# Layer 0's parameters turned by 18 transfers; layer 1's norm and statistics moved to ACT and PE, one more third of delta·x to DVE; setup transfers issued from two queues

## The chip, the cores and the metric

The kernel runs on one core of one Trainium2 chip. A core has TensorE (PE), VectorE (DVE), ScalarE (ACT), GpSimd (POOL) and SyncE (SP); SP issues nearly all transfers here. The metric is the device time in microseconds (us). The kernel before takes 19113.97 us, the median of three runs from 19105.77 to 19115.89. A smaller time is better.

## What is computed

Two blocks follow each other on 32 images of 96 channels and 56 x 56 pixels, all in float32.

- Layer 0 is an inverted bottleneck: a 1x1 convolution to 576 channels, a 3x3 depthwise convolution, squeeze-and-excite, a 1x1 convolution back to 96 channels, and the input added. Its weights are rounded to 8 bits first ("fake quant"), and its three batch norms are folded to a scale and a shift per channel.
- Layer 1 reads each image as a sequence of 3136 positions and passes it through two Mamba layers. A final 1x1 convolution is normalised over all images and positions, and layer 0's output is added again.

```python
h = (seq - mu) * rsqrt(var + EPS) * ln_g + ln_b      # per position, over 96 channels
xs, z = split(h @ in_w)                              # 192 channels each
xc = silu(causal conv of 4 taps of xs)
dt, Bm, Cm = split(xc @ xproj_w)                     # 6, 16, 16
delta = softplus(dt @ dt_w + dt_b)                   # 192 channels
hstates = scan: h = exp(delta*A) * h + delta*Bm*xc   # 192 x 16 states
y = (sum over states of hstates*Cm + Dp*xc) * silu(z)
seq = seq + y @ out_w
```

## The kernel before

The program has two phases and a short ending.

**Layer 0** takes up the first 3460 us. Weights and parameters come into SBUF, are quantised (`fake_quant`) and folded (`bn_fold`). The depthwise convolution on PE leaves the four 32-channel groups of a tile rotated by r groups, so whatever is multiplied with its result has to be rotated too: `turned` copies the scale `inv2`, the shift `sh2`, the bias `SEB2`, the weights `w3` and `sew1` with one transfer for every 32-row block. `folded` does the like for the last, half-filled tile. SP issues all of them, and behind them the first images (`load_x`). Then a loop over the images runs in an order written out by hand.

**Layer 1** is cut into units: 784 positions (`LC`) of one of 128 pieces, in one of the 2 Mamba layers, 256 units in all. A unit has 24 steps (`NT`), one for each group of 32 channels and 4 states: 192 x 16 / 128. In the order written out by hand (`manual_schedule`), each step `at` issues, engine by engine:

- `inject` (POOL): bx = u x B, for two steps at once, four steps ahead of its use.
- `decay` (ACT): da = exp(delta x A) for the next step, into one of two PSUM buffers.
- `scan` (DVE): the recurrence, for one step; `product` (DVE) multiplies 512 of the 784 columns with C for two steps at once, and `rest` (POOL) the other 272. `bring` (ACT) brings C into PSUM for `product`.
- `save` (ACT): the last state, one column for each step, if the image goes on.
- `reduce` (PE): sums the states, five steps later; `gated` (DVE) multiplies with silu(z).

Between these stand the steps of other units: `prepare(n)` has the norm, projections, convolution, delta and u of a unit, spread over the steps from -4 to 36 counted from 48 steps ahead of its own scans, so that its step 36 is issued beside step 12 of the unit ahead of it. `finish(n)` projects a finished unit and stores it. A number with a fraction in the list, such as 34.5, puts the step ahead of the scan of the next whole step. Work that waits for something holds up what is behind it on its engine.

The parts that the change touches are these. `center` subtracts the mean (PE). `square` copies the centred sequence to `xm` and squares it (ACT). `variance`, `root` and `newton` make the reciprocal root `rs`, with positions on partitions. `spread_root` lays it along the columns by a multiplication with the identity (PE), and `normalise` multiplies `xm` with it (DVE, two instructions). `conv` (PE) reads the result `xn`. `softplus` makes delta and writes it to HBM; `input_u` (POOL) multiplies two of three parts of delta and x, and `bring_x` (ACT) and `input_u0` (DVE) the first one. `spread` writes u to HBM, and `fetch` reads delta, u, B and C back, spread over the partitions as the scan wants them. `store` and `count` write a unit of the second Mamba layer to HBM, with `bn_stats` (DVE) for the last norm.

Between the two phases stands layer 1's setup, where `pieces` yields the blocks of weights that are loaded one by one from SP. All memory of layer 1's work tiles is taken up from what the setup leaves.

Of the kernel before, what the change touches and what calls it, by code (L numbers as in the profile page):

```python
# [11 lines left out]
F32 = mybir.dt.float32  # L12
AF = mybir.ActivationFunctionType
# [40 lines left out]
def conv_mamba_kernel(ctx, tc, a, out):  # L54
# [24 lines left out]
    stats = const.tile([C, B * NQ * 2, 6], F32, name="stats", tag="stats")  # L79
# [16 lines left out]
    with ExitStack() as ph:  # L96
# [19 lines left out]

        hp = loadw("hp", [128, NCT, NHP])
        w1 = loadw("w1", [C, HID])
        w3 = loadw("w3", [128, NCT, C])
        sew1 = loadw("sew1", [128, NCT, RED])  # L120
# [19 lines left out]

        fake_quant(w1, C, [HID], "w1")
# [6 lines left out]


        def turned(name, t, shape):  # L150
            to = wtile(name, [128, NSEE, *shape])
            for e, (ct, r) in enumerate(SEEN):
                if ct == FOLD:
                    parts = [(slice(h * 64, h * 64 + 64), slice(0, 64)) for h in range(2)]
                elif r == 0:
                    parts = [(slice(0, 128), slice(0, 128))]
                else:
                    parts = [
                        (slice(q * 32, q * 32 + 32), slice((q - r) % 4 * 32, (q - r) % 4 * 32 + 32)) for q in range(4)
                    ]  # L160
                for rows, src in parts:
                    sp.dma_start(to[rows, e], t[src, ct])
            return to
# [11 lines left out]

        tinv = turned("tinv", inv2.unsqueeze(2), [1])
        tsh = turned("tsh", sh2.unsqueeze(2), [1])
        tseb = turned("tseb", hp[:, :, SEB2 : SEB2 + 1], [1])
        tw3 = turned("tw3", w3, [C])
        tsew1 = turned("tsew1", sew1, [RED])  # L180
# [24 lines left out]

        xs, maps, h2s, pools, se = {}, {}, {}, {}, {}

        def load_x(b):
            if b < B:
                xs[b] = xin.tile([C, L], F32, name=f"x{b}", tag="x")  # L210
                sp.dma_start(xs[b], a["x"][b])
# [193 lines left out]
        load_x(0)  # L405
        load_x(1)
# [42 lines left out]
    with ExitStack() as ph:  # L449
# [9 lines left out]
        def loadw(name, shape, pool=wts):  # L459
            t = pool.tile(list(shape), F32, name=name, tag=name)  # L460
            sp.dma_start(t, a[name])
            return t
# [17 lines left out]
        def pieces():  # L480

            for m in range(DIN // DB):
                hc, c0 = divmod(m * DB, C)
                for h in range(2):
                    r0 = h * 64 + m % 2 * DB
                    yield slice(r0, r0 + DB), m // 2, h, slice(c0, c0 + DB), hc
# [3 lines left out]
        for to, k, h, src, hc in pieces():  # L490
            sp.dma_start(outw[to, :, k, :], a["outw"][src, :, hc, :])
            sp.dma_start(dp[to, :, k, :], a["dp"][src, :, hc, KC + 1 : KC + 3])

        araw = loadw("acol", [128, NL, NT], once)
# [48 lines left out]
        for to, k, h, src, hc in pieces():  # L543
            sp.dma_start(wbc[to, :, k, : 2 * NS], a["xpw"][src, :, hc, RANK:])
            sp.dma_start(wbc[to, :, k, 2 * NS : 2 * NS + RANK], a["xpw"][src, :, hc, :RANK])
        for h in range(2):
            for i in range(NL):
                to = wd[h * 64 + 2 * NS : h * 64 + 2 * NS + RANK, i, :, :]
                sp.dma_start(to, a["dtw"][:, i, :].rearrange("r (k m) -> r k m", k=NB))
# [27 lines left out]
        nch = B * NQ  # L577

# [17 lines left out]
        def prepare(n):  # L596
# [18 lines left out]
            def square(h):  # L615
                if h == 0:
                    d["xm"] = wt([C, LC], "xm", 1, n)
                    d["sq"] = wt([C, LC], "sq", 1, n)
                s.copy(d["xm"][:, cols(h)], d["cen", h][:C, :HB])
# [32 lines left out]
            def spread_root(h):  # L652
                ps = d["rstd", h] = bank(f"rstd_{n}_{h}")
                for k in range(NK):
                    lo, hi = max(k * TK, h * HB), min((k + 1) * TK, h * HB + HB)
                    if lo < hi:
                        pe.matmul(
                            ps[:C, lo - h * HB : hi - h * HB], d["rs"][:, k : k + 1].to_broadcast([TK, C]),
# [3 lines left out]
            def normalise(h):  # L662
                to = xn[:C, KC - 1 + h * HB : KC - 1 + h * HB + HB]
                v.tensor_mul(to, d["xm"][:, cols(h)], d["rstd", h][:C, :HB])  # L664
# [50 lines left out]
            def spread(tag, t):  # L715
# [310 lines left out]
```

## Time and profile before

| | |
|---|---|
| median of the runs | 19113.97 us |
| the profiled execution's own time | 19128.83 us |
| its span, first to last instruction | 19127.1 us |
| busy over the span | DVE 94%, POOL 81%, PE 76%, ACT 74% |
| first matmul | 112.40 us |
| scans of layer 1 | from 3563.98 us to 18828 us |
| mean granted TensorE clock | 0.816 |

Busy shares over the whole span mix stages with different limits. In the stretch from 6,000 to 12,000 us, which is layer 1 alone, DVE is busy for 5927.62 us, POOL for 5993.50, ACT for 4963.45 and PE for 4461.17. A row of groups tells an operation by its line, engine and tiles (out<-in), how many there were, the busy time, the mean length in ns, the idle time of the engine just before them and what ended that idle time. A row of a timeline has the start and the length in us, and in brackets the idle time before it. Instructions on one engine overlap a little at their ends, so the distance from start to start is what counts in a sum.

### The profile page before, as it was taken

Reading aid. Unit: us, or ns where it says so; the run is one execution under the profiler, and the core shown is the slowest. Engines: PE = TensorE matmul, PEld = TensorE weight load, DVE = VectorE, ACT = ScalarE, POOL = GpSimd, SP = SyncE. Lnnn points to the kernel's source line nnn. Section 1 sums busy time; section 2 is a strip of 40 time slices with the busy share of each in tenths; the row PEclk is TensorE's granted clock in tenths of the full one; section 3 lists DMA queues with packets and bytes.
Section 4 is the critical chain, followed back from the end, with each engine's and each line's share of the span. In section 5 each row is a group of like instructions: output and inputs, shape, how many; then the busy total and the mean of one; then the engine's idle time right before and its main releaser. Section 6 shows DMA issues by size and latency. Waiting matters only on the chain.

```text
span 19127.1 us, 282833 instructions
## 1 busy us (share of the span) xinstructions
PE 14494.5 (76%) x105692; PEld 5826.8 (30%) x105692; DVE 17929.2 (94%) x13652; ACT 14174.0 (74%) x23979; POOL 15533.5 (81%) x6638
## 2 busy tenths in 40 slices
PE   7999999777777777777777777777777777777772
PEld 3544444322222222222222222222222222222220
DVE  7888888699999999999999999999999999999993
ACT  3444444588888888888888888888888888888884
POOL 0000000599999999999999999999999999999994
PEclk9999999778777777877777787778878787777775
DMA  1000000355555555555555555555555555555557
GB/s 27 22 27 23 26 27 20 105 162 162 162 162 162 164 163 162 162 162 162 162 162 163 162 163 163 163 163 162 164 162 162 163 163 163 162 163 163 163 162 207
DMA packets 1048524, 2641.35 MB, mean 138 GB/s; under 512 B 129080, under 2 KB 342416, under 8 KB 1041000
## 3 DMA queue, kind: packets, MB, share of 16 engines
q1 hardware_dynamic: 1040488, 2584.73, 42.4%
q0 software_dynamic: 6656, 38.54, 1.0%
q8 instruction: 828, 13.57, 0.3%
q14 instruction: 552, 4.52, 0.1%
HBM read 2172.52 MB, written 449.58 MB: 137 GB/s over the span
## 4 chain that ended last, share of the span: by engine, by line
DVE 37%; issue 33%; ACT 21%; PE 5%; POOL 3%; SPq 1%; DMA 1%; POOLq 0%; DVEq 0%; ACTq 0%
DVE hh L864 20%; DVE hc L872 12%; ACT da L832 5%; ACT L588 4%; ACT L589 3%; DVE h L303 2%; ACT cp L840 2%; PE bc L701 2%; POOL bx L852 1%; ACT z L588 1%; ACT dl L588 1%; ACT xc L588 1%; PE var L625 1%; DVE z L915 1%; POOL x L378 1%
## 5 line engine op out<-in xcount | busy, mean ns | idle before, releaser
L852 POOL TENSOR_TENSOR bx<-ub,B 128x1568 f32<-128x1568 f32 x3072 | 10983.4, 3575 | 26.0 <-DMA ub<-ud 15.5
L864 DVE TENSOR_TENSOR_SCAN hh<-da,state,bx 128x784 f32<-128x784 f32 x4608 | 8315.7, 1839 | 47.5 <-ACT da L832 41.6
L832 ACT ACTIVATE da<-deltab,acol 128x784 f32<-128x784 f32 x6144 | 5631.1, 917 | 2159.5 <-DVE hh L864 2125.6
L879 POOL TENSOR_TENSOR hc<-hh,C 128x544 f32<-128x544 f32 x3072 | 4217.7, 1373 | 31.4 <-DVE hh L864 23.5
L676 PE MATMUL xs<-xn,wx 97*64 97x392 f32 x12288 | 2892.5, 607 | 1362.9 <-DVE xn L664 1362.3
L872 DVE TENSOR_TENSOR hc<-hh,cp 128x1024 f32<-128x1024 f32 x3072 | 3679.7, 1198 | 0.1
L904 PE MATMUL y<-hc,rel 128*32 128x392 f32 x24576 | 3008.2, 577 | 366.8 <-DVE hc L872 348.2
L378 POOL TENSOR_TENSOR x<-x,x 96x784 f32<-96x784 f32 x128 | 268.4, 2097 | 3180.1 <-ACT x L377 3142.2
L864 DVE TENSOR_TENSOR_SCAN hh<-da,bx 128x784 f32<-128x784 f32 x1536 | 2682.5, 1778 | 53.3 <-ACT da L832 34.2
L676 PEld LDWEIGHTS xs<-xn,wx 97*64 97x64 f32 x12288 | 1303.2, 164 | 2972.9 <-DVE xn L664 1672.6
L840 ACT COPY cp<-C 128x512 f32<-128x512 f32 x3072 | 1793.7, 584 | 372.9 <-DVE hc L872 371.1
L303 DVE SCALAR_TENSOR_TENSOR h<-hpad,hp,h 128x1568 f32<-128x1568 f32 x1024 | 2035.0, 1987 | 34.3
L701 PE MATMUL bc<-xc,wbc 64*64 64x392 f32 x3072 | 980.8, 802 | 646.7 <-ACT xc L588 646.7
L904 PEld LDWEIGHTS y<-hc,rel 128*32 128x32 f32 x24576 | 579.7, 115 | 2090.6 <-issue 1139.4
L277 PE MATMUL dw<-hpad,diag 32*32 32x392 f32 x36864 | 1113.0, 522 | 47.4 <-issue 47.1
L692 PE MATMUL z<-xn,wz 97*64 97x392 f32 x3072 | 741.2, 563 | 487.7 <-ACT xc L687 472.7
L375 PE MATMUL c<-h,w3s 128*96 128x392 f32 (+1 forms) x2560 | 968.0, 523 | 48.8 <-DVE w3s L360 48.8
L588 ACT ACT_TABLE_LOAD x768 | 985.3, 1283 | 13.5
L589 ACT ACT_TABLE_LOAD x768 | 985.3, 1283 | 11.2
L224 PE MATMUL c<-x,w 96*128 96x392 f32 x2048 | 801.9, 548 | 198.8 <-DMA x<-in_x_dram 112.4
L284 ACT ACTIVATE h<-dw,tsh,tinv 128x392 f32<-128x392 f32 x512 | 340.0, 673 | 755.8 <-PE dw L277 755.8
L774 PE MATMUL o<-z,outw 64*96 64x392 f32 x3072 | 802.9, 656 | 101.2 <-DVE z L915 100.5
(156 smaller groups left out, 15566.8 us busy)
## 6 DMA issues: line engine op xcount, KB each, us to landing
deltab<-deltad SPq DMA_DIRECT2D x1536, 392.0 KB, 5.4
ub<-ud SPq DMA_DIRECT2D x1536, 392.0 KB, 5.8
B<-bcd SPq DMA_DIRECT2D x1024, 392.0 KB, 4.2
C<-bcd SPq DMA_DIRECT2D x1024, 392.0 KB, 4.2
deltad<-dl SPq DMA_DIRECT2D x512, 294.0 KB, 3.6
ud<-us SPq DMA_DIRECT2D x512, 294.0 KB, 3.7
x<-in_x_dram SPq DMA_DIRECT2D x32, 1176.0 KB, 7.5
out_dram<-x SPq DMA_DIRECT2D x128, 294.0 KB, 2.6
```

The source lines that it names most:

```text
L303: v.scalar_tensor_tensor(acc, src, tap, acc, ALU.mult, ALU.add)
L588: s.activation(t, t, func)
L589: s.preload_act_table_set(MAIN)
L676: pe.matmul(d["xs", k][h * 64 : h * 64 + 64, :HB], wx[:, i, o, k * 64 : k * 64 + 64], xn[:, o + h * HB : o + h * HB + HB], start=o == 0, s ...
L701: pe.matmul(ps[r, :HB], wbc[r, i, k], d["xc"][r, k, :], start=k == 0, stop=k == NB - 1)
L832: s.activation(das[at][:, :LC], d["delta", k][:, p, :], AF.Exp, scale=acol[:, j, i, 2 * k + p : 2 * k + p + 1])
L840: s.copy(cps[at], data[n]["C", j][:, :LP])
L852: g.tensor_mul(bx, data[n]["u", k], beside(data[n]["B", j]))
L864: v.tensor_tensor_scan(hhs[at - p][:, p, :], das.pop(at)[:, :LC], bxs.pop(at), state[i][:, t : t + 1] if c % NQ else 0.0, ALU.mult, ALU.add,)
L872: v.tensor_mul(hcs[at - 1][:, :, :LP], hhs[at - 1][:, :, :LP], beside(cps.pop(at)))
L879: g.tensor_mul(hcs[at - 1][:, :, LP:], hhs[at - 1][:, :, LP:], beside(data[n]["C", j][:, LP:]))
L904: pe.matmul(yps[k][r0 : r0 + DB, :HB], rel, hc[:, p, h * HB : h * HB + HB], start=False, stop=j == SG - 1, skip_group_check=True,)
```

## The change

- Layer 0: the three folded vectors and the two weights stand side by side in one tile `per` (123 columns), and one loop of 18 transfers turns all of them, at most two blocks a rotation. The first two images are loaded ahead of the quantisation.
- Layer 1's setup: `pieces` yields 8 blocks, not 12, and part of the loads is issued by ACT (`s.dma_start`).
- Layer 1's norm: `turn` multiplies the sequence with the centring matrix so that positions come out on partitions (PE, 7 matmuls); there `rs` is a scale per partition, which `normalise` applies (ACT, 7 instructions); `turn_back` turns it again (PE, in `spread_root`'s place), and `normal` copies it to `xn` (ACT, two). `xm` and its two copies are gone.
- delta x: POOL keeps one third; DVE gets the second as well, by `bring_x(1)` and `input_u(1)`, at steps 38 and 39; `bring_x(0)` moves from step 36 to 34. u is written to HBM in two parts.
- Statistics: ACT takes sums and sums of squares about a pivot with accumulators (`store`); `bn_stats` is gone, and `count` moves from step 19 to 8.
- `save` copies two columns at every second step.

```diff
+        NPER = 3 + C + RED
+        per = wtile("per", [128, NCT, NPER])
+        w3, sew1 = per[:, :, 3 : 3 + C], per[:, :, 3 + C :]
...
+        load_x(0)
+        load_x(1)
+
         fake_quant(w1, C, [HID], "w1")
...
-        def turned(name, t, shape):
-            to = wtile(name, [128, NSEE, *shape])
...
-                    parts = [
-                        (slice(q * 32, q * 32 + 32), slice((q - r) % 4 * 32, (q - r) % 4 * 32 + 32)) for q in range(4)
-                    ]
-                for rows, src in parts:
-                    sp.dma_start(to[rows, e], t[src, ct])
-            return to
+        for o, t in enumerate((inv2, sh2, hp[:, :, SEB2])):
+            v.tensor_copy(per[:, :, o], t)
+
+        turn = wtile("turn", [128, NSEE, NPER])
...
+                parts = [(slice(r * 32, 128), slice(0, 128 - r * 32)), (slice(0, r * 32), slice(128 - r * 32, 128))]
+            for rows, src in parts:
+                sp.dma_start(turn[rows, e], per[src, ct])
...
-            for m in range(DIN // DB):
-                hc, c0 = divmod(m * DB, C)
+            for k, c, o, hc, c0 in ((0, 64, 0, 0, 0), (1, DB, 0, 0, 64), (1, DB, DB, 1, 0), (2, 64, 0, 1, DB)):
...
             sp.dma_start(outw[to, :, k, :], a["outw"][src, :, hc, :])
-            sp.dma_start(dp[to, :, k, :], a["dp"][src, :, hc, KC + 1 : KC + 3])
-
-        araw = loadw("acol", [128, NL, NT], once)
+            s.dma_start(dp[to, :, k, :], a["dp"][src, :, hc, KC + 1 : KC + 3])
+
+        araw = loadw("acol", [128, NL, NT], once, s)
...
-            sp.dma_start(wbc[to, :, k, 2 * NS : 2 * NS + RANK], a["xpw"][src, :, hc, :RANK])
+            s.dma_start(wbc[to, :, k, 2 * NS : 2 * NS + RANK], a["xpw"][src, :, hc, :RANK])
...
-                sp.dma_start(to, a["dtw"][:, i, :].rearrange("r (k m) -> r k m", k=NB))
+                s.dma_start(to, a["dtw"][:, i, :].rearrange("r (k m) -> r k m", k=NB))
...
-                s.copy(d["xm"][:, cols(h)], d["cen", h][:C, :HB])
                 s.activation(d["sq"][:, cols(h)], d["cen", h][:C, :HB], AF.Square)
...
+            def turn(m):
+                ps = d["ct", m] = bank(f"ct_{n}_{m}")
+                for k in TURNS[m]:
+                    o = (k - TURNS[m][0]) * C
+                    pe.matmul(ps[:TK, o : o + C], seqs[c, i][:, k * TK : (k + 1) * TK], cen, start=True, stop=True)
+
+            def normalise(m):
...
+                    s.activation(d["xt"][:, k, :], d["ct", m][:TK, o : o + C], AF.Copy, scale=d["rs"][:, k : k + 1])
+
+            def turn_back(h):
...
-                            ps[:C, lo - h * HB : hi - h * HB], d["rs"][:, k : k + 1].to_broadcast([TK, C]),
+                            ps[:C, lo - h * HB : hi - h * HB], d["xt"][:, k, :],
...
-            def normalise(h):
+            def normal(h):
                 to = xn[:C, KC - 1 + h * HB : KC - 1 + h * HB + HB]
-                v.tensor_mul(to, d["xm"][:, cols(h)], d["rstd", h][:C, :HB])
+                s.copy(to, d["xn", h][:C, :HB])
...
+            def input_u(k):
+
+                if k == NB - 1:
+                    d["us"] = wt([128, NB, HB], "us", 1, n)
+                    g.tensor_mul(d["us"][:, k], d["dl"][:, k], d["xc"][:, k])
+                    return
+                v.tensor_mul(d["us"][:, k], d["dl"][:, k], d["up", k][:, :HB])
+                spread("u", d["us"], slice(0, 1) if k == 0 else slice(1, NB))
...
-                steps += [(8 + h + then, lambda h=h: spread_root(h)), (11 + then, lambda h=h: normalise(h))]
+                steps += [(7 + h + then, lambda h=h: turn(h)), (8 + h + then, lambda h=h: normalise(h))]
+                steps += [(9 + h + then, lambda h=h: turn_back(h)), (10 + h + then, lambda h=h: normal(h))]
...
-            steps += [(26.5 + then, lambda: through(d["z"], AF.Silu)), (34.5 + then, softplus), (35 + then, input_u)]
-            steps += [(36 + then, bring_x), (36 + then, input_u0)]
+            steps += [(26.5 + then, lambda: through(d["z"], AF.Silu)), (34.5 + then, softplus), (35 + then, lambda: input_u(NB - 1))]
+            steps += [(34 + then, lambda: bring_x(0)), (36 + then, lambda: input_u(0))]
+            steps += [(38 + then, lambda: bring_x(1)), (39 + then, lambda: input_u(1))]
...
+                s.activation(
+                    d["pre"][:, cols(h)], d["o", h][:C, :HB], AF.Identity, bias=g2[:, b : b + 1],
+                    accum_out=stats[:, 0, at : at + 1],
+                )
...
+                s.activation(squares, d["pre"][:, cols(h)], AF.Square, bias=pivot, accum_out=stats[:, 1, at : at + 1])
...
-                    for h in range(2):
-                        v.bn_stats(stats[:, 2 * c + h, :], d["pre"][:, cols(h)])
...
-                (6, lambda: store(0)), (7, lambda: store(1)), (19, count),
+                (6, lambda: store(0)), (7, lambda: store(1)), (8, count),
...
-            if c % NQ + 1 < NQ:
-                s.copy(state[i][:, t : t + 1], hh[:, p, LC - 1 :])
+            if place(t)[2] == 1:
+                hh = hhs.pop(at - 1)
+                if c % NQ + 1 < NQ:
+                    s.copy(state[i][:, t - 1 : t + 1], hh[:, :, LC - 1])
...
-        v.bn_aggr(mv, stats.rearrange("p n k -> p (n k)"))
+        off = one.tile([C, 1], F32, name="off", tag="off")
+        v.tensor_reduce(mv, stats, AX.X, ALU.add)
```

## The prediction

> **What bounds the kernel now.** I read the page's groups first, then the waits of layer 1, then the timelines of single engines. Most of the span is layer 1. From 4,000 to 18,500 us the groups count 4,404 + 1,440 scans of DVE, so a unit of 24 scans takes 14,500 / 5,844 x 24 = 59.55 us, and 256 units 15,245 us.
>
> ```profile
> L852 POOL TENSOR_TENSOR bx<-ub,B 128x1568 f32<-128x1568 f32 x243 | 860.0, 3539 | 0.0
> L879 POOL TENSOR_TENSOR hc<-hh,C 128x544 f32<-128x544 f32 x243 | 322.6, 1328 | 0.0
> L726 POOL TENSOR_TENSOR us<-dl,xc 128x784 f32<-128x784 f32 x20 | 36.8, 1839 | 0.0
> ```
>
> These are POOL's groups from 3,800 to 5,000 us, early in layer 1, with no idle time at all. Each instruction begins 0.032 us before its forerunner ends, so a unit costs POOL 12 x (3.539 + 1.328) + 1.839 - 25 x 0.032 = 59.44 us. Later POOL has built up a lead: its bx ends some 4 us ahead of the scan that reads it (it was 1.7 us in the first 16 units), and its hc starts as little as 0.14 us after its scan. So it waits a little for DVE, inside its recorded spans.
>
> ```profile
> DVE us L734 <- ACT up L731: 98.5, 244, 0.5
> DVE hh L864 <- ACT da L832: 63.4, 191, 0.6
> ```
>
> DVE's own waits, 4,000 to 18,500 us: never for POOL, twice per unit for ACT. With two short ones DVE's idle time is 0.72 us a unit, leaving 59.55 - 0.72 = 58.83 us of work. DVE with its waits for ACT sets the pace; POOL's 59.44 is only 0.11 behind. Relieving one alone would win almost nothing.
>
> ```profile
> 10036.45 1.85 DVE L864 TENSOR_TENSOR_SCAN hh<-da,state,bx 128x784 f32<-128x784 f32 x1
> 10038.21 1.01 DVE L664 TENSOR_TENSOR xn<-xm,rstd 96x392 f32<-96x392 f32 x2
> 10039.14 1.84 DVE L864 TENSOR_TENSOR_SCAN hh<-da,state,bx 128x784 f32<-128x784 f32 x1
> 10040.90 1.19 DVE L872 TENSOR_TENSOR hc<-hh,cp 128x1024 f32<-128x1024 f32 x1
> 10042.33 0.56 DVE L734 TENSOR_TENSOR us<-dl,up 128x392 f32<-128x392 f32 x1 [0.24 <-ACT up L731]
> 10042.81 0.56 DVE L915 TENSOR_TENSOR z<-z,y 128x392 f32<-128x392 f32 x1
> ...
> 10058.88 1.01 DVE L789 BATCH_NORM_STATS2 stats<-sq 96x6 f32<-96x392 f32 x2
> 10059.81 1.83 DVE L864 TENSOR_TENSOR_SCAN hh<-da,state,bx 128x784 f32<-128x784 f32 x1
> ```
>
> DVE's timeline: prices from start to start. The xn pair costs 0.93 us (10,039.14 - 10,038.21), us 0.48, a pair of statistics 0.93. A scan costs 1.75 and a product 1.11.
>
> ```profile
> 66.45 18.94 SPq L162 DMA_DIRECT2D tw<-w  x30
> 85.44 19.01 SPq L162 DMA_DIRECT2D tsew<-sew  x30
> 104.49 1.52 SPq L211 DMA_DIRECT2D x<-in_x_dram  x3
> ```
>
> SP's start: 0.63 us for each transfer, the images last; they land at 112.40, where PE's first matmul begins.
>
> **Start: -90 us.** 150 turning transfers become 18, and x is issued behind nine loads, at about 5 us. Landed 7.9 us later (112.40 - 104.49) it is hidden: the first matmul next waits for w1, whose quantisation ends on DVE at 21.48, and three added copies of 128x5 cost 0.15 each. So 112.4 becomes 22.0. What is late next? The turned tile: quantised w3 ends near 24.4, then 18 x 0.63 = 11.3, and 3.7 for a landing (u's stores), in all 39.5. Its first reader, layer 0's first activation of a PE tile, came 20.2 us after the first matmul (132.64 - 112.40), so at 42.2, and needs only 7 of the 18. Were all 3 us later than that, it would cost just the excess.
>
> **Setup of layer 1: -14 us.** SP issued 53 blocks of weights every 0.64 us, acol 25th, at 3476.89; PE's chain from acol (3478.98) to its last setup matmul took 13.4, while the sequence's load went out at 3495.25. Now SP keeps 16 and ACT has 21: acol is ninth on ACT's queue, at about 3463.5 and landed by 3465.5, so PE is done near 3479. The sequence's load waits for this, as it is placed in the setup's memory; 3479 + 3.3 = 3482 in place of 3498.6, less 2 for the longer first norm chain. ACT had 18 us of idle time here, and nothing but acol's exponential queues behind its issues. [...] With transfers as the limit the gain would be 0; but DMA engines are 24% busy from 3,420 to 3,600 us and issues stand 0.64 apart, so issue time is what is short. I take 14, range 0 to 19.
>
> **Loop, DVE.** Out: xn 0.93, statistics 0.93 / 2 = 0.47 (only the second layer has them). In: the second third of u, 0.48. 58.83 - 0.93 - 0.47 + 0.48 = 57.91 us, plus waits for ACT.
>
> **Loop, POOL.** u falls from 784 to 392 columns. 544 columns take 1.328 and 1568 take 3.539, that is 2.16 ns each and 0.15 fixed (784: 1.85, seen 1.84), so 1.00 us; 59.44 - 0.84 = 58.60 us. POOL becomes the longer one.
>
> **Loop, ACT.** It is busy 82% of the loop, some 49 us a unit. Out: two xm copies (0.38 each from start to start), half of the state copies (12 x 0.09 in three units of four). In: two copies to xn and one for up (0.38 each); seven activations of 96 columns; in half of the units two squares (0.4) and four accumulator reads (0.1 from start to start). The 96-column price has no row: the 1-column state copy is 0.18 long and spaced 0.09, a 392-column copy 0.48 and 0.38, so 0.165 by the line between, 1.16 for seven. [...] Sum about +1.3 us, 86% of the new unit: no bound, but it bunches.
>
> ```profile
> 10035.46 0.92 ACT L832 ACTIVATE da<-deltab,acol 128x784 f32<-128x784 f32 x1 [0.82 <-DVE hh L864]
> 10036.58 0.59 ACT L840 COPY cp<-C 128x512 f32<-128x512 f32 x1 [0.20 <-DVE hc L872]
> 10037.18 1.28 ACT L588 ACT_TABLE_LOAD   x1
> ...
> 10040.97 0.92 ACT L832 ACTIVATE da<-deltab,acol 128x784 f32<-128x784 f32 x1
> 10041.83 0.47 ACT L731 COPY up<-xc 128x392 f32<-128x392 f32 x1
> ```
>
> Around softplus (ACT's timeline, T = 10,035.34, the end of scan 10) I walk the new order. Softplus and its two table loads end at T + 5.63. `up` now stands ahead of it, so us no longer waits; but `normal(1)` (0.38) and a state copy come between it and da of step 13, ready at T + 7.0. DVE, without xn, wants it at T + 6.65: a wait of 0.35 in the place of 0.40. Behind `normal(1)`, PE's convolution starts at T + 6.1, not T + 3.5. After such idle time PE ran it at 0.86 us a matmul rather than 0.49 and needed 5 us, so to T + 11.1. ACT's copy of its result queues at about T + 9.7, holds up da of step 16 until T + 12.9, and DVE wants that at T + 13.9. The last third's convolution is late by 2.9 and meets the next table switch, which costs about 0.26, as now. DVE: 57.91 + 0.35 + 0.26 = 58.5 us.
>
> u's second part leaves after step 15 of DVE, T + 13.9, and SP's later fetches queue behind it. Two stores, then B, delta, u, C, delta, u: the last six took 9.7 us from issue to landing in the trace (10,046.46 to 10,056.12), so T + 24.9. POOL wants u at T + 25.8, DVE at T + 34. Hidden by 1 us, and by more once DVE is ahead of POOL. PE gets 7 more matmuls of 96 columns (about 0.25 each as the spreads have), with 15 us idle a unit to hide them.
>
> Both engines near one length wait for one another a little: 58.70 us, a gain of 0.85 x 256 = **218 us**.
>
> **End: -8 us.** The aggregate (7.08) and DVE's statistics (1.04) go; a reduction of 512 columns (0.7), four small operations (0.7) and about 1.5 of squares come, and 2.2 of wait ahead of the aggregate shrinks.
>
> Sum: 90 + 14 + 218 + 8 = 330; 19,127 - 330 = 18,797 in a profiled execution. The runs' median lies 15 below its own time (19,128.8), so **18,783 us**.
>
> **Rivals.**
> 1. Less gain in the loop, chance 0.18: ACT's bunched work makes waits that eat half. For it: da has two buffers and the walk left 1 us. Against it: ACT mostly waits for DVE. Unit 59.2, total -202: about 18,910.
> 2. More gain, 0.13: POOL's 3.54 for bx holds interference that eases; its shortest is 3.48. Then 58.60 - 12 x 0.055 = 57.94, DVE with fewer waits 58.1: total -483, about 18,630. Against it: DVE's waits have no reason to vanish.
> 3. The start isn't shortened, as something else holds the first matmul (0.03 within the likeliest): the rest alone, about 18,870.
> 4. Slower, 0.04: ACT's copy of the first convolution (step 14) waits for PE, and da is stuck behind it. To end 38 us late the loop must lose the 112 of the other parts and 38 more, 0.59 a unit: 60.14, DVE waits of 2.2 and not 0.6. With 1 us of slack, PE must come 2.6 us later than in my walk. For it: the slow matmuls after idle time. Against it: turning works PE shortly before, so it may be faster.
>
> **How the numbers follow.** The likeliest case has 0.63: units of 58.5 to 59.0, 18,710 to 18,860. No change has 0.02. The range takes in half of rival 2 and most of rival 1: 18,670 to 18,905. A measurement tells 0.2%, 38 us, from no change. Faster 0.94, same 0.02, slower 0.04.
>
> **What would show it.** First matmul near 22 us; sequence landed near 3,392 (earlier by both parts); units of 58.7; POOL without idle time and DVE idle more, now also for bx; us without its wait for up. Wrong if DVE's waits for da exceed 1 us a unit, ACT waits for PE's xs, or POOL waits for u's landing.

## The result and the profile after

The kernel after takes 18961.83 us, the median of four runs (18937.42 to 18969.25); the kernel before took 19114.93 beside it (19105.77 to 19127.98). The ratio is 0.9917 with a 95% interval of 0.990 to 0.9934. So 153 us were won where 331 were forecast, and the time lies 57 us above the range.

The profiled execution of after has a span of 18935.6 us (own time 18937.42, the fastest of the four), 191.5 less than before's 19127.1. Cut at the same events, the two traces differ so:

| stretch | before, us | after, us | difference | predicted |
|---|---|---|---|---|
| start to the first matmul | 112.40 | 21.99 | -90.4 | -90 |
| layer 0, to PE's last matmul of its gate | 3348.2 | 3320.9 | -27.3 | 0 |
| setup, to PE's first matmul on the sequence | 38.0 | 21.9 | -16.1 | -16 |
| from there to the first scan | 65.4 | 74.3 | +8.9 | +2 |
| first scan to the end of the last | 15264.1 | 15200.2 | -63.9 | -218 |
| from there to the end | 299.0 | 296.3 | -2.7 | -8 |

Layer 0's 27 us can't be put down to the change. In the thirteen experiments, which all keep after's layer 0 as it is, this stretch takes 3320.8 to 3350.3 us; it differs by that much from one execution to the next, and the 3348.2 of before lie within that. Without it the stretches give 164 us. What is missing is in the loop: a unit takes 59.31 us (mean of 224 units, from scan 384 to scan 5,760), where it took 59.55 and 58.70 was forecast.

The start as forecast: the first rows of PE's timeline of after, with the start and the length in us.

```profile
21.99 13.08 PE L229 MATMUL c<-x,w 96*128 96x392 f32 x32 [21.99 <-DVE w L146]
```

And SP's timeline: the images are issued early, and 18 turning transfers take 11.35 us.

```profile
5.49 0.82 SPq L153 DMA_DIRECT2D x<-in_x_dram  x2
...
24.36 11.35 SPq L178 DMA_DIRECT2D turn<-per  x18
```

POOL's groups of after, 4,000 to 18,500 us (244.5 units), with the mean length in ns and the idle time ahead:

```profile
L877 POOL TENSOR_TENSOR bx<-ub,B 128x1568 f32<-128x1568 f32 x2934 | 10453.0, 3563 | 84.1 <-DMA ub<-ud 40.8 <-POOL hc L904 27.1 <-issue 12.7
L904 POOL TENSOR_TENSOR hc<-hh,C 128x544 f32<-128x544 f32 x2934 | 3981.5, 1357 | 60.6 <-DVE hh L889 55.2 <-issue 0.2
L749 POOL TENSOR_TENSOR us<-dl,xc 128x392 f32<-128x392 f32 x245 | 253.0, 1033 | 0.0
```

POOL's part of u costs 1.03, as forecast (1.00), and POOL now has idle time, 0.58 us a unit. It isn't the bound. DVE's waits in the same stretch (total us, times, longest):

```profile
DVE hh L889 <- ACT da L857: 314.3, 579, 1.6
```

That is 1.29 us a unit, where before it was 0.26 for da and 0.40 for `up`. DVE's own work is 59.31 - 1.36 of idle time = 57.95 us, and 57.91 was forecast. So DVE's work was priced rightly as a sum, and its waits for ACT have doubled. ACT's own waits say for whom it is late; before, `xc` waited 1.4 us in the whole stretch:

```profile
ACT xc L701 <- PE xs L690: 870.8, 638, 2.7
ACT da L857 <- DVE hh L889: 740.3, 1568, 1.2
```

ACT stands 3.6 us a unit in front of the convolution's results, up to 2.7 at a time. One unit shows how. T is the end of scan 10, 9,998.65 here. First PE's timeline:

```profile
9998.67 1.54 PE L930 MATMUL y<-hc,rel 128*32 128x392 f32 x8
10004.79 5.53 PE L690 MATMUL xs<-xn,wx 97*64 97x392 f32 x16 [4.58 <-DVE us L751]
10010.25 1.57 PE L925 MATMUL y<-xc,dd 64*64 64x392 f32 x4
10011.75 1.53 PE L930 MATMUL y<-hc,rel 128*32 128x392 f32 x8
10013.21 3.09 PE L690 MATMUL xs<-xn,wx 97*64 97x392 f32 x16
...
10017.03 2.86 PE L690 MATMUL xs<-xn,wx 97*64 97x392 f32 x16
```

PE starts the convolution at T + 6.1, exactly where the walk had it, and runs it cold. That time in four stretches, each with its length, PE's busy time, the granted clock, and the transfers' share and GB/s:

```profile
10004.79:10007.50 2.71, 2.71 (x10) 0.50 0.95 248
10007.50:10010.30 2.80, 2.80 (x12) 0.50 0.02 6
10010.30:10013.20 2.90, 2.90 (x13) 0.50 0.00 0
10013.20:10016.30 3.10, 3.10 (x24) 0.92 0.81 194
```

The clock stays at 0.50 for 8.4 us, though PE is busy throughout. The sums of y behind the first third pay too: eight take 1.53 us here, and 0.86 at the full clock behind the second third. This unit is among the longest. Over the 224 units PE works at 0.50 for 3.6 to 9.0 us from the start of the convolution, 5.7 in the median. ACT's timeline of the same unit:

```profile
10002.91 1.28 ACT L591 ACT_TABLE_LOAD   x1
...
10004.30 0.47 ACT L678 COPY xn<-xn 96x392 f32<-96x392 f32 x1
...
10010.35 0.48 ACT L701 COPY xc<-xs 128x392 f32<-128x392 f32 x1 [1.87 <-PE xs L690]
...
10016.35 0.49 ACT L701 COPY xc<-xs 128x392 f32<-128x392 f32 x1 [2.69 <-PE xs L690]
...
10019.93 0.48 ACT L701 COPY xc<-xs 128x392 f32<-128x392 f32 x1 [0.83 <-PE xs L690]
...
10022.43 1.28 ACT L590 ACT_TABLE_LOAD   x1
```

And what DVE makes of it, on its timeline (scans 13 and 14, 18, 21 and 22):

```profile
10005.63 3.47 DVE L889 TENSOR_TENSOR_SCAN hh<-da,bx 128x784 f32<-128x784 f32 x2 [0.42 <-ACT da L857]
...
10017.76 1.79 DVE L889 TENSOR_TENSOR_SCAN hh<-da,bx 128x784 f32<-128x784 f32 x1 [0.85 <-ACT da L857]
...
10027.26 3.47 DVE L889 TENSOR_TENSOR_SCAN hh<-da,bx 128x784 f32<-128x784 f32 x2 [1.63 <-ACT da L857]
```

The copy to `xn` (10,004.30) comes behind softplus's second table load; three copies of `xc` then wait for PE; ACT comes late to the next table switch (10,022.43); and scan 21, behind that switch, waits 1.63 here. Over the 224 units the mean idle time ahead of scan 13 is 0.30, of 18 0.11, and of 21 0.86.

### The profile page after: what moved, and what is told of

Same layout as the page of the kernel before. It is cut to its first block, busy times and chain, and to the rows that moved or that the text cites. A ratio compares the mean times of both kernels' runs of the same rounds, so it can differ in the third digit from the quotient of the medians.

```text
span 18935.6 us, 291237 instructions
## 1 busy us (share of the span) xinstructions
PE 15002.3 (79%) x109276; PEld 6041.9 (32%) x109276; DVE 17699.9 (93%) x13147; ACT 14621.6 (77%) x24492; POOL 15355.8 (81%) x6638
## 4 chain that ended last, share of the span: by engine, by line
issue 36%; DVE 27%; ACT 18%; PE 9%; POOL 7%; DMA 2%; SPq 0%; DVEq 0%; POOLq 0%; ACTq 0%
DVE hc L897 12%; DVE hh L889 12%; ACT da L857 5%; PE xs L690 5%; POOL bx L877 4%; ACT L590 3%; ACT L591 2%; DVE h L308 2%; ACT cp L865 2%; POOL hc L904 2%; DMA C<-bcd 1%; ACT z L590 1%; PE y L930 1%; ACT z L701 1%; ACT xc L590 1%
## 5 line engine op out<-in xcount | busy, mean ns | idle before, releaser
L904 POOL TENSOR_TENSOR hc<-hh,C 128x544 f32<-128x544 f32 x3072 | 4168.2, 1357 | 76.2 <-DVE hh L889 67.8
L690 PE MATMUL xs<-xn,wx 97*64 97x392 f32 x12288 | 2813.0, 611 | 1284.8 <-DVE us L751 1284.8
L690 PEld LDWEIGHTS xs<-xn,wx 97*64 97x64 f32 x12288 | 995.6, 165 | 3074.3 <-DVE us L751 1531.9
L715 PE MATMUL bc<-xc,wbc 64*64 64x392 f32 x3072 | 878.1, 728 | 542.5 <-ACT xc L590 542.5
L671 PE MATMUL xn<-eye,xt 112*96 112x112 f32 (+1 forms) x4096 | 743.6, 350 | 433.6 <-ACT xt L664 432.3
L701 ACT COPY xc<-xs 128x392 f32<-128x392 f32 x768 | 372.1, 485 | 915.6 <-PE xs L690 915.6
L590 ACT ACT_TABLE_LOAD x768 | 985.3, 1283 | 13.5
L793 PE MATMUL o<-z,outw 64*96 64x392 f32 x3072 | 862.4, 699 | 96.4 <-DVE z L941 96.2
L289 ACT ACTIVATE h<-dw,turn 128x392 f32<-128x392 f32 x512 | 340.1, 673 | 731.8 <-PE dw L282 731.8
```

Source lines behind the costliest of these rows:

```text
L590: s.activation(t, t, func)
L690: pe.matmul(d["xs", k][h * 64 : h * 64 + 64, :HB], wx[:, i, o, k * 64 : k * 64 + 64], xn[:, o + h * HB : o + h * HB + HB], start=o == 0, s ...
L904: g.tensor_mul(hcs[at - 1][:, :, LP:], hhs[at - 1][:, :, LP:], beside(data[n]["C", j][:, LP:]))
```

## Experiments

My theory after this: the convolution is late, because `normal(1)` stands behind softplus on ACT and because PE has gone cold, and ACT carries this lateness into the switch for the Silu of xc. Two rivals: ACT has simply too much work, or POOL sets the pace. A unit is measured as above, in one execution; "idle" is per unit. Each ratio is to runs of the kernel before taken beside that kernel.

| kernel | median, us | ratio to before (95%) | unit | DVE idle | POOL idle |
|---|---|---|---|---|---|
| after | 18961.8 | 0.9917 (0.9900-0.9934) | 59.31 | 1.36 | 0.58 |
| norm_early | 18819.1 | 0.9839 (0.9824-0.9853) | 58.78 | 0.84 | 0.10 |
| norm_early_skip | 18813.2 | 0.9836 (0.9821-0.9850) | 58.77 | 0.83 | 0.09 |
| warm | 18825.2 | 0.9844 (0.9829-0.9858) | 58.84 | 0.89 | 0.13 |
| early_warm | 18818.0 | 0.9838 (0.9823-0.9853) | 58.77 | 0.83 | 0.08 |
| conv1_first | 18848.2 | 0.9862 (0.9847-0.9876) | 58.89 | 0.95 | 0.22 |
| skip_bank | 18941.4 | 0.9907 (0.9890-0.9923) | 59.31 | 1.35 | 0.57 |
| old_norm | 19578.6 | 1.0237 (1.0220-1.0254) | 61.86 | 2.82 | 3.13 |
| old_norm2 | 19056.7 | 0.9965 (0.9952-0.9978) | 59.73 | 0.85 | 1.12 |
| early_u_pool | 18986.0 | 0.9927 (0.9910-0.9943) | 59.48 | 1.62 | 0.00 |
| early_stats_dve | 18875.1 | 0.9868 (0.9853-0.9882) | 58.99 | 0.63 | 0.29 |
| early_save | 18824.7 | 0.9852 (0.9837-0.9866) | 58.83 | 0.91 | 0.15 |
| early_u_sbuf | 20383.6 | 1.0660 (1.0642-1.0677) | 64.96 | 0.82 | 6.23 |
| one_queue | 18963.8 (one run) | | 59.31 | 1.36 | 0.58 |

### The copy ahead of softplus (norm_early)

```diff
-                steps += [..., (10 + h + then, lambda h=h: normal(h))]
+                steps += [..., (10 + 0.5 * h + then, lambda h=h: normal(h))]
```

> The second half of the normalised sequence (ACT's copy normal(1), step 11) goes ahead of softplus and its two table loads instead of behind them; nothing else changes. Theory 'late convolution': ACT stands 3.6 us a unit before the convolution's banks because PE starts the convolution only after that copy, at 10,004.8 in the unit shown, and cold. With the copy ahead of softplus PE starts some 4 us earlier and after less idle time, ACT's waits for xs fall below 1.5 us a unit, DVE's waits at steps 21 and 45 (behind the Silu of xc) fall from 0.94 to about 0.3; softplus is 0.38 later, so the wait at step 13 grows from 0.39 to about 0.7. Unit 59.31 - 0.64 + 0.3 = 58.97, 256 units: -87 us, about 18,875 us. Rival 'ACT is simply overloaded' (seven short activations at 0.25, squares, accumulator reads): the order doesn't matter, unit 59.3, about 18,960. Rival 'POOL sets the pace': unit 59.3, the waits only move from ACT to POOL.

Measured: 143 us less than after, a unit of 58.78. ACT's waits for xs are gone from the list (0.5 us in the whole loop), and DVE's waits, in the same stretch of the trace of norm_early:

```profile
DVE hh L889 <- ACT da L857: 194.7, 553, 2.3
```

The idle time ahead of scan 21 fell from 0.86 to 0.41; ahead of scan 13 it grew only from 0.30 to 0.33. The unit gained more than expected. The theory holds; both rivals said 59.3.

### PE kept warm (warm, and both: early_warm)

```diff
+            def warm():
+                for _ in range(16):
+                    pe.matmul(
+                        yps[0][:TK, 400:512], eye[:TK, :TK], eye[:TK, :TK], start=True, stop=True,
+                        skip_group_check=True,
+                    )
...
+            if n > 4 and not then:
+                steps += [(11, warm)]
```

> The kernel after with 16 extra matmuls of 112 columns at step 11, into columns of y's bank that nothing reads, so that PE is not idle while ACT does softplus; the order on ACT is that of the kernel after, and the convolution still waits for normal(1). It tells the part of the cold PE from the part of the order. Theory 'late convolution': the first third takes 2.9 us and not 5.5, the sums of y behind it 1.7 and not 3.1, so ACT has the second third 4 us earlier; ACT's waits for xs fall from 3.6 to about 1 us a unit, DVE's at steps 21 and 45 from 0.94 to about 0.35; unit 58.7, 256 x 0.6 = 154 us, about 18,810 us. If the cold clock is the smaller part: xs0 faster, but the waits at 21 and 45 stay above 0.6, about 18,890. Rivals 'ACT overloaded' and 'POOL': PE's time doesn't matter, 59.3, about 18,960.

> norm_early and warm together. Each alone took the unit from 59.31 to 58.78 and 58.84. If the two worked on one wait, and what is left is set by POOL (58.67 without its idle time): 58.7 to 58.8, about 18,815 us, the same as norm_early. If order and cold clock were separate losses that add: 59.31 - 0.53 - 0.47 = 58.3, about 18,700 us.

Measured: with nothing changed on ACT, and PE burdened with more work, 137 us less than after. The convolution starts at the same place (T + 6.3 in the median), and its first third ends at T + 9.1, not 11.6. Both cures together give what one gives: they work on the same wait. norm_early alone doesn't part the two causes, as with its earlier start PE is warm in most units. But not in all: in 74 of the 224 units the first third still runs at a clock of 0.50 (5.5 us in the place of 2.9), and scan 21 waits no longer there than in the others (0.39 and 0.42). In warm 14 units still have the late start and the cold clock; scan 21 waits 1.15 in them, and 0.45 in the other 210. So the loss needs the two causes at once, a late start and a cold clock.

### Which third is late (conv1_first, skip_bank, norm_early_skip)

```diff
-                steps += [(t, lambda k=k: conv(k, (0, 1))), (t + 1, lambda k=k: conv(k, (2, 3)))]
+                early_by = (0, 1, 0)[k]
+                steps += [(t - early_by, lambda k=k: conv(k, (0, 1))), (t + 1 - 2 * early_by, lambda k=k: conv(k, (2, 3)))]
```

> The kernel after, with PE doing the second third of the convolution right behind the first (both halves at step 13) and the sums of y of step 14 behind it; the order on ACT and the start of the convolution are unchanged. It tells which third's lateness costs DVE. If the last third sets the loss, as PE's work up to its end is the same: ACT's wait for the second third (up to 2.7 us) turns into a longer wait for the last one, the wait of DVE at step 18 (0.15 us a unit in the mean) goes, those at steps 21 and 45 stay near 0.85; unit 59.15, about 18,920 us. If the second third sets it: waits at 21 and 45 fall to 0.4, unit 58.8, about 18,825 us.

Measured: 58.89, near the value for "the second third". But the run brought the last third earlier too, to T + 19.2 from 19.8, so it doesn't part the two. That PE's work up to the end of the last third is the same left out the clock: from the start of the convolution it stays at 0.50 for 4.8 us in the median, and for 5.7 in after. In the unit of conv1_first shown here it is up after 5.5 us, in that of after above after 8.4.

```profile
9979.90:9982.60 2.70, 2.70 (x10) 0.50 0.95 248
9982.60:9985.40 2.80, 2.80 (x12) 0.50 0.02 6
9985.40:9988.20 2.80, 2.80 (x19) 0.98 0.00 0
```

Either PE's speed had brought the last third earlier, or the PSUM bank that ACT's earlier copy set free. That bank alone was changed next, in after (skip_bank) and on top of norm_early (norm_early_skip):

```diff
                 if taps[0] == 0:
+                    if k == NB - 1:
+                        bank(f"skip_{n}")
                     d["xs", k] = bank(f"xs_{n}_{k}")
```

> The kernel after, with one of the two rotating PSUM banks passed over ahead of the last third's convolution (as in norm_early_skip, here without moving normal(1)). In the unit shown of the kernel after, PE began the last third at 10,017.03, just behind ACT's copy of the second third (10,016.35 to 10,016.83), which frees the bank; with the other bank it needs only DVE's second part of u (10,012.3) and can start behind the sums of y, near 10,017. If the bank holds the last third up: waits at steps 21 and 45 fall from 0.85 to 0.6, unit 59.1, about 18,910 us. If PE's own cold work up to there is what is late: no change within 0.1 a unit, about 18,950 us.

> As norm_early, and in addition one bank of the two rotating PSUM banks is passed over ahead of the last third's convolution, so that this third takes the bank that DVE's second part of u released (step 15) and not the one that ACT's copy of the second third releases (step 16). In the kernel after, the added bank for the second part of u shifted this rotation. Theory 'late convolution' with the bank as a part of it: the last third starts up to 3 us earlier than in norm_early and warm, DVE's waits at steps 21 and 45 fall below 0.3, unit 58.7 to 58.8, about 18,825 us. If the bank doesn't matter: as norm_early, within 0.05 us a unit. Rivals 'ACT overloaded' and 'POOL': 59.3, about 18,960.

Measured: the unit is 59.31 with it as without, and 58.77 against 58.78 on top of norm_early; the bank doesn't matter. The table has the medians over 224 units, in us from T: when PE starts the convolution, when each third is ready, when ACT copies it, and when the table load for the Silu of xc begins.

| kernel | start | ready | copied | table load |
|---|---|---|---|---|
| before | 3.4 | 9.0, 13.4, 17.0 | 10.9, 15.5, 19.9 | 22.5 |
| after | 6.3 | 11.6, 16.2, 19.8 | 11.7, 16.3, 19.9 | 22.4 |
| norm_early | 2.2 | 5.1, 11.2, 16.8 | 9.8, 14.3, 19.4 | 22.0 |
| warm | 6.3 | 9.1, 13.5, 17.1 | 9.8, 14.3, 19.4 | 22.0 |
| conv1_first | 6.3 | 11.5, 14.1, 19.2 | 11.5, 14.8, 19.4 | 22.0 |

Undisturbed, ACT wants the thirds at 9.8, 14.3 and 19.4. The kernel after delivers each of them late, by 1.8, 1.9 and 0.4; before, the last one was ready 2.9 ahead of its copy. The lateness of the last copy is small, but it comes right ahead of the switch.

The units of after tell which third counts. In 84 of the 224 ACT doesn't wait for the last third, though it has waited 1.1 us for the second, and scan 21 waits 0.33. In the 111 in which ACT waits over 0.5 us for the last third, scan 21 waits 1.23. So the last third makes the switch late. The second one's lateness goes with the 0.11 ahead of scan 18, which are gone in conv1_first.

### What the new norm is worth (old_norm, old_norm2)

```diff
-                steps += [(7 + h + then, lambda h=h: turn(h)), (8 + h + then, lambda h=h: normalise(h))]
-                steps += [(9 + h + then, lambda h=h: turn_back(h)), (10 + h + then, lambda h=h: normal(h))]
+                steps += [(8 + h + then, lambda h=h: spread_root(h)), (11 + then, lambda h=h: normalise(h))]
```

with `spread_root`, `normalise` and `xm` as before; old_norm2 besides has

```diff
-            steps += [(34 + then, lambda: bring_x(0)), (36 + then, lambda: input_u(0))]
+            steps += [(36 + then, lambda: bring_x(0)), (36 + then, lambda: input_u(0))]
```

> The kernel after with the norm of the kernel before (two ACT copies of the centred sequence, PE spreads the root, DVE multiplies twice at step 11), the rest as after. Theory 'late convolution': DVE's two multiplications do not wait for softplus, PE starts earlier, and the wait at steps 21 and 45 falls from 0.94 to about 0.26; DVE gets 0.93 us of work back: 58.03 + 0.93 + 0.39 + 0.26 = 59.6, +0.3 a unit, about 19,040 us; the norm's change was worth only 0.3 us a unit of the 0.93 that DVE was relieved of. Rival 'ACT overloaded': ACT is relieved by about 1.7 us of short activations and gets two copies back (0.76); DVE's waits go by half: 58.96 + 0.65 = 59.6 too, but with ACT's waits for xs unchanged at about 3.6 us a unit. Rival 'POOL sets the pace': unit 59.3 as now, with DVE idle for bx less than before.

> As old_norm, but the copy of xc for the first part of u is put back behind softplus (step 12), where the kernel before has it. In old_norm ACT stood in front of that copy until DVE's xn at step 11 gave its PSUM bank free, and softplus stood behind it. Theory 'late convolution': with that wait gone only the norm's own price is left. DVE has 57.95 + 0.93 = 58.88 us of work and the waits of the kernel before, 0.72: unit 59.6, about 19,035 us; so the new norm as it stood in the kernel after brought 0.3 us a unit of DVE's 0.93. If the new norm's late convolution cost more than it won: unit below 59.31, under 18,962. Rival 'ACT overloaded': DVE's waits fall below 0.4, unit 59.2.

old_norm is slower than before, which nobody expected. ACT's waits in its trace:

```profile
ACT up L732 <- DVE xn L667: 963.1, 234, 4.2
```

`bring_x(0)` at step 34 needs the PSUM bank that DVE's `normalise` frees one step later, and softplus stands behind it: 4.1 us lost on ACT in each unit. The parts of the change are thus not independent; the earlier copy of xc is possible only with the new norm. old_norm2 gives the norm's own worth: 59.73 (59.6 expected), DVE's work 59.73 - 0.85 = 58.88, as worked out. Against norm_early's 58.78 the new norm, with `bring_x(0)` in the place that each norm allows, is worth 0.95 a unit, all of DVE's 0.93; in the kernel after it brings only 0.42.

### The other two parts of the loop (early_u_pool, early_stats_dve)

```diff
-                    g.tensor_mul(d["us"][:, k], d["dl"][:, k], d["xc"][:, k])
+                    g.tensor_mul(d["us"][:, 1:], d["dl"][:, 1:], d["xc"][:, 1:])
...
-                spread("u", d["us"], slice(0, 1) if k == 0 else slice(1, NB))
+                spread("u", d["us"], slice(0, NB))
...
-            steps += [(38 + then, lambda: bring_x(1)), (39 + then, lambda: input_u(1))]
```

> As norm_early, with two thirds of u back on POOL (one DVE part and one store for all of u, as in the kernel before); DVE has 0.48 less. In norm_early POOL is idle 0.10 us a unit of 58.78. Theory 'POOL now sets the pace in norm_early, DVE with its waits just behind': POOL 58.67 + 0.84 = 59.5, unit 59.5, 256 x 0.73 = +187, about 19,005 us. Rival 'DVE and ACT set it': DVE is relieved by 0.48, unit 58.3 to 58.8.

Measured: 59.48 (59.5 expected), with POOL's groups, 4,000 to 18,500 us, free of idle time:

```profile
L876 POOL TENSOR_TENSOR bx<-ub,B 128x1568 f32<-128x1568 f32 x2926 | 10353.7, 3539 | 0.0
L903 POOL TENSOR_TENSOR hc<-hh,C 128x544 f32<-128x544 f32 x2926 | 3893.0, 1330 | 0.0
L749 POOL TENSOR_TENSOR us<-dl,xc 128x784 f32<-128x784 f32 x244 | 451.0, 1848 | 0.0
```

And DVE waits for POOL, which in norm_early it does only once, for 0.9 us:

```profile
DVE hh L888 <- POOL bx L876: 237.5, 432, 1.3
```

So POOL sets the pace there, and its floor with one third of u is 59.48 - 0.84 = 58.64: norm_early is within 0.14 us of it.

early_stats_dve takes the squares and sums off ACT and has, on top of norm_early,

```diff
                 if i + 1 == NL:
+                    for h in range(2):
+                        v.bn_stats(stats[:, 2 * c + h, :], d["pre"][:, cols(h)])
...
-                (6, lambda: store(0)), (7, lambda: store(1)), (8, count),
+                (6, lambda: store(0)), (7, lambda: store(1)), (19, count),
```

> As norm_early, with the statistics as in the kernel before: bn_stats twice on DVE in the second layer's units at step 19, no squares and no accumulator reads on ACT. DVE 57.95 + 0.47 = 58.42 a unit with 0.84 of waits left as they are: 59.2, +0.45 a unit, about 18,930 us. Rival 'ACT overloaded': ACT is 0.8 us a unit lighter, DVE's waits fall to about 0.5 and the unit stays at 58.9 or below, about 18,850 us.

Measured: 58.99, between the two. In every second unit, the one in which the two `bn_stats` are issued at step 19, DVE's idle time ahead of scan 21 is gone (0.40 in norm_early); in the others it stays at 0.40. The two instructions stood just ahead of that scan and gave ACT the time for its table loads. Taking away 0.47 of work there won only 0.21.

### Two attempts at more (early_save, early_u_sbuf)

Both on top of norm_early. early_save issues `save` ahead of the early steps, and so ahead of the table switches; early_u_sbuf gives DVE the second part of xc from SBUF, without the copy to PSUM.

```diff
+                if 0 <= at - 2 < total:
+                    save(at - 2)
                 for step in early.get(at, ()):
                     step()
...
-                if 0 <= at - 2 < total:
-                    save(at - 2)
```

```diff
-                d["up", k] = bank(f"up_{n}_{k}")
-                s.copy(d["up", k][:, :HB], d["xc"][:, k])
+                if k == 0:
+                    d["up", k] = bank(f"up_{n}_{k}")
+                    s.copy(d["up", k][:, :HB], d["xc"][:, k])
...
-                v.tensor_mul(d["us"][:, k], d["dl"][:, k], d["up", k][:, :HB])
+                v.tensor_mul(d["us"][:, k], d["dl"][:, k], d["xc"][:, k] if k else d["up", k][:, :HB])
```

> norm_early, with the copy of the states (0.09 us from start to start) ahead of the table switches on ACT instead of between a switch and the next da. DVE's waits at steps 13, 21, 37 and 45 shrink by 0.09 each, 0.18 a unit, from 58.78 to 58.60 if DVE with its waits sets the pace; POOL's own work in early_u_pool was 59.48 without idle time, so 59.48 - 0.84 = 58.64 is the floor: unit 58.65 to 58.70, 18,795 us. If POOL sets the pace already at 58.78: no change, 18,819.

> norm_early, with DVE's second part of u reading xc straight from SBUF: no copy on ACT (0.4 us) and no PSUM bank for it. If DVE and POOL don't hinder one another with two SBUF operands on DVE: DVE's us stays at 0.48, unit 58.7, about 18,800 us. If the operand's place matters, DVE's us takes up to twice as long (0.9) and POOL's bx beside it is stretched by as much: 58.78 + 0.4 = 59.2, about 18,920 us.

early_save won nothing (58.83 against 58.78), and it could not: the copy of the state is still ahead of the da that DVE waits for, only on the other side of the switch. ACT's timeline of norm_early, then of early_save, around the switch for the Silu of xc:

```profile
9975.76 0.59 ACT L865 COPY cp<-C 128x512 f32<-128x512 f32 x1 [0.19 <-DVE hc L897]
...
9980.16 0.19 ACT L913 COPY state<-hh 128x2 f32<-128x2 f32 x1
9980.26 0.91 ACT L857 ACTIVATE da<-deltab,acol 128x784 f32<-128x784 f32 x1
```

```profile
9968.74 0.59 ACT L865 COPY cp<-C 128x512 f32<-128x512 f32 x1 [0.19 <-DVE hc L897]
9969.26 0.19 ACT L913 COPY state<-hh 128x2 f32<-128x2 f32 x1
...
9973.26 0.92 ACT L857 ACTIVATE da<-deltab,acol 128x784 f32<-128x784 f32 x1
```

From the copy of C to da it is 4.50 us in the one and 4.52 in the other. What a shorter chain on ACT would bring thus stays open. early_u_sbuf lost 6.2 us a unit, far outside both expectations. Its timeline, DVE and POOL:

```profile
10065.27 3.60 POOL L878 TENSOR_TENSOR bx<-ub,B 128x1568 f32<-128x1568 f32 x1
...
10067.72 6.43 DVE L752 TENSOR_TENSOR us<-dl,xc 128x392 f32<-128x392 f32 x1
...
10068.84 1.33 POOL L905 TENSOR_TENSOR hc<-hh,C 128x544 f32<-128x544 f32 x1
10070.14 3.60 POOL L878 TENSOR_TENSOR bx<-ub,B 128x1568 f32<-128x1568 f32 x1
10074.08 1.84 DVE L890 TENSOR_TENSOR_SCAN hh<-da,state,bx 128x784 f32<-128x784 f32 x1
```

The multiplication that takes 0.55 us with one operand in PSUM takes 6.43 with both in SBUF. It ends 0.4 after the second bx, when POOL has nothing ready.

### The setup (one_queue)

```diff
-        araw = loadw("acol", [128, NL, NT], once, s)
+        araw = loadw("acol", [128, NL, NT], once)
...
-            s.dma_start(wbc[to, ...], ...)
+            sp.dma_start(wbc[to, ...], ...)
```

and likewise for `dp` and `dtw`.

> The kernel after with all setup transfers of layer 1 issued by SP, as in the kernel before; the rest as after. From PE's last matmul of layer 0's gate to the first one on the sequence it is 21.9 us in the kernel after and 38.0 in the kernel before. If the second queue made this difference: 36 to 38 us here (the two-row blocks of the kernel after save a few issues). If the fewer, larger blocks did: about 22 us. The loop is unchanged, 59.3 a unit.

Measured: 30.3 us from the last matmul of the gate (the second of the two in the first row, at 3,356.55) to the sequence's first, between the two expectations. PE's timeline of one_queue:

```profile
3356.38 0.48 PE L404 MATMUL gp<-gp,fusw 96*96 96x1 f32 x2 [0.35 <-ACT gp L403]
...
3386.88 2.90 PE L615 MATMUL cen<-seq,cen 96*96 96x392 f32 x4 [3.72 <-DMA seq<-out_dram]
```

Of the 16 us won, about 8 are the second queue's; the other 8, by difference, fall to the larger blocks. The loop is the same to 0.01 us.

## Why the prediction was wrong

**Right.** The start: 21.99 for 22.0, and layer 0 did not begin to wait for the turned tile. The setup up to the sequence: 16.1 for 16. DVE's work: 57.95 for 57.91. The wait for softplus: 0.30 for 0.35. POOL's share of u: 1.03 for 1.00; u's second part lands in time but for 0.17 us a unit of waits for it (40.8 over 244.5 units). POOL, which was to become the longer engine, has idle time instead (0.58), and DVE doesn't wait for bx. The walk around softplus was right as far as it went: convolution from T + 6.3 (6.1), first third to 11.6 (11.1), its copy wanted at 9.8 (9.7), scan 16 without a wait.

**The step that failed** is the sentence after it: "The last third's convolution is late by 2.9 and meets the next table switch, which costs about 0.26, as now." The lateness was right, 17.0 to 19.8. The cost was taken over from the trace of before without asking when ACT would want that third (19.4), and the second third (wanted at 14.3, ready at 16.2) was left out of the walk. ACT then reaches the switch late, and scan 21 waits 0.86 a unit, not 0.26. The idle time ahead of scan 18 adds 0.11. These 0.71 are the error; the 0.2 allowed for two engines of near length, against 0.10 of other short waits, and smaller terms take 0.10 off. The unit is 59.31 in place of 58.70, and 0.61 x 256 = 156 of the 179 us by which the forecast was too low. The three signs named for being wrong all came: waits for da over 1 us a unit (1.29), ACT's waits for xs (3.6), POOL's for u (0.17).

Even that 0.26 was no property of the switch. It was mostly a mean over two kinds of units: in before, the idle time ahead of scan 21 is 0.39 in every second unit and none in the others, in which `bn_stats` covers it. The change took this cover away, so the wait without any lateness is 0.40, as norm_early shows; early_stats_dve brings the cover back and the wait goes. norm_early runs a unit of 58.78: without the late convolution the forecast of 58.70 would have been off by 0.08. That is luck in part: the wait ahead of scan 21 is 0.15 longer there than forecast, and the allowance of 0.2 is nearly as much too large.

**The rivals.** The first, less gain by ACT's bunched work, came nearest (unit 59.2) with another mechanism; norm_early and warm, which leave ACT all its work, speak against that one. The fourth had the mechanism: ACT's copy of the convolution waits for PE. It looked at step 14 only, and demanded 2.6 us more of lateness before the whole gain would be lost. Its reassurance, that the turning works PE shortly before, was wrong: PE idles 4.58 us after the turning and the sums, and the clock is 0.50.

**Small terms.** From the sequence to the first scan it takes 8.9 us longer, not 2; 4.4 of them go with norm_early (69.9 for 74.3). The end: the coefficients are ready 15.2 us after the last scan and not 22.2, so 7.0 were won as foreseen (8). But the transfers behind them, with DMA engines 89% busy from 18,800 to 19,127 us before, took 4 us longer, and in all runs this stretch takes 295.5 to 300.1 us; the gain can't be told from that spread.

**Two prices weighed.** For the seven activations of 96 columns I took 0.165 us each, an estimate from the line between two rows of before's trace (1 and 392 columns). The trace of after has them 0.22 apart (four in 1.00 us, the last 0.33 long), so ACT's work grew by 1.7 us a unit and not 1.3 (busy 51.0 for 49.3, 4,000 to 18,500 us). It cost nothing, as it fell where ACT waits for DVE (from scan 8 to scan 10 ACT idles 1.54 us in before and 0.42 in after, means of 224 units): warm and norm_early keep all seven and run a unit of 58.84 and 58.78. In the setup I held that issue time was short and not the transfers, from issues 0.64 us apart and DMA engines 24% busy; one_queue bears this out for 8 us: with SP alone issuing, the stretch takes 30.3 us and not 21.9.

## What to carry to other kernels

When a step is moved behind something, don't stop the walk at the first deadline that it keeps: for each later piece of it, write down when it will be ready and when its in-order reader wants it, up to the next point where that reader has no slack. A wait's present price is a price with its present cover, so look for the instruction that stands just ahead of it, and ask whether the change removes it. And a part that must wait for a busy engine's long operation belongs ahead of it in the order: here one number in a list was worth 143 us, nearly as much as the whole change.

## What the runs showed that was not expected

- A DVE multiplication with both inputs in SBUF, beside a POOL that works without a pause, took 6.7 us in the median of 256 (early_u_sbuf) in place of 0.55. In 252 of the 256, POOL's next two instructions began while DVE's was pending, and DVE's came to its end only when POOL had run out of work; in the unit shown above it ended 0.41 us after the second of them, and POOL's next one had waited 5.20. What holds DVE back meanwhile the trace doesn't show. The copy of xc to PSUM, which looks like waste, is what keeps DVE out of this: with it, in norm_early, the multiplication takes 0.55. That the copy of C does the like was not tried.
- How long PE's granted clock stays at 0.50 under uninterrupted work differs from unit to unit: 3.6 to 9.0 us in after, counted from the start of the convolution. One unit's clock says little of the others'.
- Sixteen matmuls a unit that nothing reads, in 250 of the units, made the kernel 0.7% faster than the kernel after.
